# A gated, quantized feed-forward on one core: inner seven-product splits for two of each slot's products in the last batch, with the work around them put anew

## The chip, the cores and the metric

The kernel runs on one core of a Trainium2 chip. Its engines work side by side, each through its own list of instructions in order: TensorE (PE) multiplies 128x128 weights with moving tokens, VectorE (DVE), ScalarE (ACT) and GpSimd (POOL) do the elementwise work, and SyncE (SP) issues the transfers. The metric is the device time of one execution in microseconds; the time before is the median of three runs.

## The reference

For x of 4 batches x 1024 tokens x 512 and a condition vector of 128 per batch, with up weights of 4096x512 and down weights of 512x2048:

```python
scale = cond @ norm_w.T + 1.0
ms = mean(x * x, axis=-1, keepdims=True)
h = x * (scale[:, None, :] * rsqrt(ms + 1e-6))
u = h @ up_w.T
val, gate = split(u, 2, axis=-1)
h = val * gelu(gate, approximate=False)
hq = act_quant(h)        # per token: s = 127/clip(max|h|, 1e-5); clip(round(h*s), -128, 127)/s
wq = weight_quant(down_w)  # ternary, with one scale for the matrix
y = hq @ wq.T
return y + x
```

## The kernel before, in words

The work goes batch by batch (b = 0 to 3), each of 1024 tokens in two halves of 512. A batch has 16 slots, one for every 128 gate columns and the 128 value columns that go with them; slot g is number g mod 16 of batch g // 16. Slots 48 to 63 are the last batch.

In a slot the up-projection of a 2x2 block matrix is done with seven products in place of eight (Strassen's scheme in Winograd's form). Tokens and weights are kept as sums and differences, each as a high and a low fp16 part, so a product c is six matmuls of 512 columns (`product`, L703): two weight parts by two token parts without low by low, times two blocks of the inner dimension. The methods of `Slot` name them: `first` (c = 0) starts bank A; `fourth` (c = 4) starts bank E; `second`, `third`, `fifth`, `gate` and `value` add to A, E and B, a copy of A. A slot has 42 matmuls of 512 columns. `slot` writes them in this order: first, fourth and second of the current slot, third of the one before, fifth, gate of the one before, value. `third_out` (L840) and `value_out` (L860) multiply value by gelu(gate) into the buffer H; `gate_sum` (L848), `value_sum` (L857) and the copies lie between.

The weights of a slot come from a DRAM scratch (s_dram) into one of two buffers, SXY, some of them through a transposing DMA (L489) and some plain (L491), all in SP's queue. The tokens of the next batch, in R, are written by four "turns" per batch (L678), transposing DMAs on the same queue.

While a batch's slots run, DVE and ACT quantize the batch before. `pair_max` takes the maximum over two slots (L906, L911, then L913); `token_max` brings the maximum over the partitions together on POOL (L927); `token_scale` (L932, L938) makes 1/scale on 128x512 numbers; then H is scaled (L993) and rounded, either on DVE (L997) or by two passes of ACT (L1001, L1005). A planner (`Filler`) hands these to the places x, y and z of a slot by their costs, after the due place of each. z is the end of the slot. The quantized batch is multiplied with the ternary weights (also with seven products, `Pair`; L1049 to L1058 make sums, L1070 the matmuls, L1118 the evictions) in slots 10 to 13 of batches 1 and 2, and for batch 2 after slot 63: this last stretch is called the tail. There the last batch's maximum, scale and rounding are done too, with `token_row`, which moves the maxima to 16 partitions by 32 (L949), `token_fold`, which scales them there (L955, L956), and a broadcast over the partitions (L962). The ending matmuls are po_end (L1022).

PSUM has banks by tag: A, E (two each), B (one), and "po" (three), which the down-projection uses.

Of the kernel before, what the change touches and what calls it, by code (L numbers as in the profile page):

```python
# [19 lines left out]
P = 128  # L20
# [7 lines left out]
X_UP = 2.0**8  # L28
# [23 lines left out]
def glu_quant_kernel(  # L52
# [33 lines left out]
    DVE.memset(undo_up, 1.0 / W_UP)  # L86
# [406 lines left out]
    LOADS = ((Y_TO, C_ALL), (0, Y_FROM, True), (Y_FROM + 1, Y_TO), (Y_FROM, Y_FROM + 1, True))  # L493

    def s_load_x(g):
        s_load(g, *LOADS[0])
        s_load(g, *LOADS[1])

# [199 lines left out]
    def product(c, g, ps, start, stop):  # L698
# [3 lines left out]
        for n, (w, l, k) in enumerate(TERMS):  # L702
# [98 lines left out]
    class Slot:  # L801

        def __init__(self, g):
            self.g = g

        def first(self):
            self.A = bank("A", 2, name=f"A_{self.g}")
            product(0, self.g, self.A, True, True)

        def first_copy(self):  # L810
            self.B = bank("B", 1, name=f"B_{self.g}")
            ACT.copy(self.B, self.A)  # L812

        def fourth(self):
            self.E = bank("E", 2, name=f"E_{self.g}")
# [20 lines left out]
        def third(self):  # L836
            product(3, self.g, self.A, False, True)
# [6 lines left out]
        def gate(self):  # L844
            product(2, self.g, self.E, False, True)
# [13 lines left out]
        def value_out(self):  # L859
            DVE.scalar_tensor_tensor(  # L860
                h_half(self.g, 1), self.v, gain(self.g, 0), self.t2, ALU.mult, ALU.mult
            )

# [88 lines left out]
    def token_fold(h, few):  # L952

        row = wpool.tile([P, TOK], F32, name=f"row_{h}", tag="gm", bufs=1)[0:1]
# [35 lines left out]
    def quant_scale(b, i, h, s):  # L990
        v, _ = grid_of(b, i, h)
        r = s[:, h * TOK : (h + 1) * TOK].rearrange("p (o t) -> p o t", o=1)
        DVE.tensor_tensor(v, v, r.to_broadcast([P, 2, TOK]), ALU.mult)  # L993
# [551 lines left out]

    state = {}
    for b in range(1, B):
# [8 lines left out]
        last_pair = NJ // 2 - 1  # L1556
        for h in range(2):
            add_pair(
                dve, act, b - 1, last_pair, h, (0, "xz"[h]),
                lambda now, h=h: token_max(b - 1, h, am),  # L1560
            )
        for h in range(2):
            for cost, f in token_scale(h, am):
# [3 lines left out]
        add_pieces(dve, act, b - 1, am, PIECES, (2, "x"))  # L1567
        for i in range(NJ // 2 - 1):
            for h in range(2):
                add_pair(dve, act, b, i, h, (2 * i + 3, "x"))  # L1570
        steps = {}
        pairs = {}
        if b == 1:
            steps[1, "z"] = [(d_total, (0.1, 0))]
        if b + 1 < B:
# [25 lines left out]
        for j in range(NJ):  # L1601
            g = b * NJ + j
            down = b + 1 < B and j in DOWN
# [12 lines left out]

            def run(p):
                nonlocal left
                for f, _ in steps.get((j, p), ()):
# [4 lines left out]
                elif p == "z":  # L1624
                    left = dve.run((j, p), left)
                if p != "z":
# [18 lines left out]
            if j + 1 == min(DOWN):  # L1645
                mid[0] = more_sums
            if down:
# [201 lines left out]
```

## Time and profile before

| | |
|---|---|
| median of 3 runs | 712.53 us (711.96 to 712.65) |
| span of the profiled execution | 710.3 us |
| outside the span | 2.23 us against the median |
| PE, DVE, ACT, POOL busy | 703.8, 593.1, 421.9, 155.0 us |
| matmuls of 512 columns in a slot of the last batch | 42 |

The page is of one profiled execution. Each row of the groups gives a line, an engine, an operation, what it writes and reads with shapes, how many there are, their busy time with the mean of one in ns, and the idle time before them with what ended it. Rows of a timeline give the start, the length and the same description.

### The profile page before, as it was taken

What the parts mean: (1) busy time and instruction counts of PE and PEld (TensorE: products, weight loads), DVE (VectorE), ACT (ScalarE), POOL (GpSimd) and SP (SyncE); (2) the same over time, 40 slices, a digit from 0 to 9 for tenths busy, and PEclk for the clock granted to TensorE, in tenths of its full rate; (3) what the DMA queues carried; (4) which work ended last, traced back from release to release, by engine and by line L of the source; (5) the groups of instructions that cost most, each with busy time, mean ns of one, the idle gap of its engine ahead of it and who ended that gap; (6) DMA issues with size and microseconds to landing.
All of it is one profiled execution on the core that took longest, in us unless ns stands there. A gap on an engine that the chain in (4) does not pass through costs nothing.

```text
span 710.3 us, 10162 instructions
## 1 busy us (share of the span) xinstructions
PE 703.8 (99%) x3620; PEld 355.3 (50%) x3620; DVE 593.1 (84%) x881; ACT 421.9 (59%) x714; POOL 155.0 (22%) x162
## 2 busy tenths in 40 slices
PE   8999999999999999999999999999999999999998
PEld 4544444444444446664444446665444444445854
DVE  7999878899888799998798868977688888755896
ACT  6987798975777754534336675544334665332473
POOL 1444535551200405430200033440020000000120
PEclk9999999999999999999999999999999999999999
DMA  7989999899776766479344555786744444442253
GB/s 261 324 270 252 254 188 263 217 207 227 264 135 163 179 178 172 136 174 225 118 118 105 133 126 150 191 188 141 207 105 105 104 105 97 99 101 90 105 178 119
DMA packets 223188, 120.26 MB, mean 169 GB/s; under 512 B 185353, under 2 KB 194589, under 8 KB 223138
## 3 DMA queue, kind: packets, MB, share of 16 engines
q1 hardware_dynamic: 222986, 119.49, 65.7%
q8 instruction: 28, 0.46, 0.3%
q14 instruction: 22, 0.18, 0.1%
q10 hardware_dynamic: 152, 0.13, 0.1%
HBM read 52.32 MB, written 23.09 MB: 106 GB/s over the span
## 4 chain that ended last, share of the span: by engine, by line
PE 97%; DVE 1%; ACT 1%; DMA 1%; issue 0%; ACTq 0%; SPq 0%
PE A L703 43%; PE E L703 21%; PE B L703 11%; PE po L1070 9%; PE po_end L1022 4%; PE pg L718 3%; PE pv L718 3%; PE pz L1194 1%; DMA s_dram<-s_rows 1%; PE ptx L1178 1%; PE pv L791 0%; PE po_B L1070 0%; PE pg L791 0%; PE pw L388 0%; PE po_E L1070 0%
## 5 line engine op out<-in xcount | busy, mean ns | idle before, releaser
L703 PEld LDWEIGHTS <-SXY 128*128 128x128 f16 x2268 | 221.9, 98 | 260.3
L703 PE MATMUL A<-R,SXY 128*128 128x512 f16 x1170 | 270.7, 379 | 0.0
L703 PE MATMUL E<-R,SXY 128*128 128x512 f16 x606 | 147.1, 379 | 0.0
L840 DVE SCALAR_TENSOR_TENSOR H<-A,sg,t 128x512 f32<-128x512 f32 x59 | 44.2, 749 | 61.2 <-PE A L703 56.9
L703 PE MATMUL B<-R,SXY 128*128 128x512 f16 x324 | 78.8, 379 | 0.0
L993 DVE TENSOR_TENSOR H<-H,am 128x1024 f32<-128x1024 f32 x64 | 76.5, 1217 | 0.0
L851 ACT ACTIVATE t<-t,sg 128x512 f32<-128x512 f32 x59 | 42.5, 719 | 57.0 <-DVE t L848 56.9
L911 DVE TENSOR_REDUCE gm<-H 128x512 f32<-128x1024 f32 x56 | 69.3, 1237 | 1.0
L927 POOL PARTITION_ALL_REDUCE am<-R x8 | 14.3, 1793 | 228.8 <-DVE R L913 228.8
L834 ACT ACTIVATE t<-B,sg 128x512 f32<-128x512 f32 x59 | 40.5, 686 | 36.9 <-PE B L703 36.9
L827 ACT COPY t<-A 128x512 f32<-128x512 f32 x59 | 34.3, 581 | 43.3 <-PE A L703 42.5
L820 ACT COPY v<-E 128x512 f32<-128x512 f32 x59 | 34.6, 586 | 33.5 <-PE E L703 30.0
L860 DVE SCALAR_TENSOR_TENSOR H<-v,sg,t 128x512 f32<-128x512 f32 x59 | 47.1, 800 | 7.3 <-ACT t L851 6.9
L812 ACT COPY B<-A 128x512 f32<-128x512 f32 x59 | 33.8, 573 | 32.4 <-PE A L703 32.0
L857 DVE TENSOR_TENSOR v<-A,v 128x512 f32<-128x512 f32 x59 | 40.4, 685 | 14.9 <-PE A L703 13.0
L1070 PE MATMUL po<-wd,R 128*128 128x256 fp8e4 x416 | 52.4, 273 | 0.0
L1070 PEld LDWEIGHTS <-R 128*128 128x128 bf16 (+1 forms) x448 | 43.8, 98 | 8.9
L848 DVE TENSOR_TENSOR t<-E,t 128x512 f32<-128x512 f32 x59 | 39.9, 678 | 6.6 <-PE E L703 6.6
L913 DVE TENSOR_TENSOR R<-R,gm 128x512 f32<-128x512 f32 x56 | 41.7, 745 | 1.1
L578 POOL TENSOR_SCALAR ssq<-ssq 128x2 f32<-128x2 f32 x12 | 5.4, 451 | 164.1 <-ACT xt L608 116.1
L1001 ACT ACTIVATE H<-H 128x1024 f32<-128x1024 f32 x33 | 34.7, 1051 | 5.2 <-DVE H L993 5.2
L1005 ACT ACTIVATE R<-H 128x1024 bf16<-128x1024 f32 x33 | 34.8, 1056 | 0.7
(249 smaller groups left out, 928.2 us busy)
## 6 DMA issues: line engine op xcount, KB each, us to landing
SXY<-s_dram SPq DMA_DIRECT2D x45, 256.0 KB, 3.0
SXY<-s_dram SPq DMA_DIRECT2D x51, 128.0 KB, 3.1
xr<-in_x_dram SPq DMA_DIRECT2D x19, 256.0 KB, 3.0
out_dram<-xr SPq DMA_DIRECT2D x19, 256.0 KB, 2.6
H<-in_L_cond_up_w_dram SPq DMA_DIRECT2D x9, 512.0 KB, 4.3
H<-in_x_dram SPq DMA_DIRECT2D x8, 512.0 KB, 6.2
s_dram<-s_rows SPq DMA_DIRECT2D x16, 256.0 KB, 2.7
s_dram<-SXY SPq DMA_DIRECT2D x4, 896.0 KB, 4.5
```

The lines of the kernel that those rows point to most:

```text
L703: PE.matmul(o, s[:, w, k, :], operand(g // NJ, c, l, k), start=start and n == 0, stop=stop and n == len(TERMS) - 1, skip_group_check=True,)
L718: PE.matmul(ps, a[k // 2][:, w, k % 2, :], XP[:, l, k, h * TOK : (h + 1) * TOK], start=n == 0, stop=n == len(terms) - 1,)
L834: ACT.activation(self.t1, self.B, AF.Gelu, scale=gain(self.g, 1))
L840: DVE.scalar_tensor_tensor(h_half(self.g, 0), self.A, gain(self.g, 0), self.t1, ALU.mult, ALU.mult)
L848: DVE.tensor_tensor(self.t2, self.E, self.t2, ALU.add)
L851: ACT.activation(self.t2, self.t2, AF.Gelu, scale=gain(self.g, 1))
L857: DVE.tensor_tensor(self.v, self.A, self.v, ALU.add)
L860: DVE.scalar_tensor_tensor(h_half(self.g, 1), self.v, gain(self.g, 0), self.t2, ALU.mult, ALU.mult)
L911: DVE.tensor_reduce(gm[0], v, AX.X, ALU.max, apply_absolute_value=True)
L913: return [largest, lambda: DVE.tensor_tensor(m, m, gm[0], ALU.max)]
L993: DVE.tensor_tensor(v, v, r.to_broadcast([P, 2, TOK]), ALU.mult)
L1070: PE.matmul(po, w[:, j], m, start=start and j == 0, stop=stop and j == n - 1, skip_group_check=True,)
```

## The change

1. *Slots 4 to 13 of the last batch, in five pairs.* Products 0 and 4 of two neighbouring slots are four blocks with the same tokens. A second seven-product scheme goes over them: two slots by two halves of the inner dimension, two halves of the 512 tokens. A product is then three matmuls of 256 columns, and the two products of two slots, before 24 matmuls of 512 columns, are 42 of 256 (`Inner`, `two_slots`). Sums of tokens are made once for the batch (`two_tokens`); sums of weights for every pair on POOL, with a cast by ACT between (`two_weights`); the raw weights come by transfers of their own (`two_load`). `lower_left` and `lower_right` are additions of 256 columns on DVE. `p0` stands for product 0 of a pair, `p4` for product 4. The steps of both slots' other products are written out by hand in `two_slots`.
2. *A hand-written plan for the last batch.* TWO_PLAN names the slot and place of each piece of quantization in place of the planner. Four scalings go to POOL ("pool scale", L1238), two maxima are taken over four slots at once ("four"), rounds go to ACT ("up", "down"). One maximum (slots 12 and 13, second half) is moved behind slot 63, ahead of `token_fold`.
3. *The third batch's token scales* are made as the tail does it: a row of 16 by 32 numbers, scaled there and broadcast by POOL.
4. *The first weight sums* of the pairs, with their loads and the first token sums, are made at the end of batch 2.
5. Slot 62 takes its banks A and E from the "po" banks; the scale of the tokens X_UP goes from 2^8 to 2^7, and `undo_up` with it.

On SP, at the end of batch 2. Before:

```order
L1113 DMA out_0_dram<-xr_1_1_3_4544 128x512
L678 DMA_TRANSPOSE R_78<-nx_3_2_4602 128x28x128
L678 DMA_TRANSPOSE R_78<-H_79 128x28x128
L491 DMA SXY_81<-s_dram_84 128x1024
L491 DMA SXY_81<-s_dram_84 128x1536
```

Now:

```order
L1358 DMA out_0_dram<-xr_1_1_3_4544 128x512
L687 DMA_TRANSPOSE R_78<-nx_3_2_4602 128x28x128
L912 DMA two_r0_4696<-s_dram_84 128x512 x2
L914 DMA_TRANSPOSE two_r1_4697<-s_dram_84 128x4x128 x2
L687 DMA_TRANSPOSE R_78<-H_79 128x28x128
L491 DMA SXY_81<-s_dram_84 128x1024
L491 DMA SXY_81<-s_dram_84 128x1536
```

Four transfers of raw weights now stand between the last two token turns of the last batch, and the loads of slot 48 behind them.

On DVE, around the end of slot 53 (the next pair is 54 and 55). A_53, E_53, v_53 and t2_53 are slot 53's banks and buffers. Before:

```order
L857 TENSOR_TENSOR v_53_5190<-A_53_5174,v_53_5190 128x512
L860 SCALAR_TENSOR_TENSOR H_79<-v_52_5121,sg_3_4828,t2_52_5149 128x512
L993 TENSOR_TENSOR H_79<-H_79,am_2_4830 128x2x512
L997 TENSOR_SCALAR R_78<-H_79 128x4x256
L977 RECIPROCAL dq_3_4831<-dq_3_4831 128x8
L978 TENSOR_SCALAR dq_3_4831<-dq_3_4831,wmean_105 128x8
L840 SCALAR_TENSOR_TENSOR H_79<-A_53_5174,sg_3_4828,t1_53_5198 128x512
L993 TENSOR_TENSOR H_79<-H_79,am_2_4830 128x2x512 x2
L997 TENSOR_SCALAR R_78<-H_79 128x4x256
L848 TENSOR_TENSOR t2_53_5218<-E_53_5183,t2_53_5218 128x512
```

Now, with `lower_left` (L1017) and `lower_right` (L1020) of the next pair:

```order
L872 TENSOR_TENSOR v_53_5149<-A_53_5148,v_53_5149 128x512
L1238 TENSOR_TENSOR H_79<-H_79,am_2_4852 128x2x512
L1242 TENSOR_SCALAR R_78<-H_79 128x4x256
L863 TENSOR_TENSOR t2_53_5287<-E_53_5289,t2_53_5287 128x512
L1017 TENSOR_TENSOR A_55_5330<-Z0_54_5328,uv_54_5332 128x256
L1020 TENSOR_TENSOR A_55_5330<-A_54_5326,uv_54_5332 128x256
L1017 TENSOR_TENSOR v_55_5331<-Z4_54_5327,two_n_4695 128x256
L1020 TENSOR_TENSOR v_55_5331<-E_54_5329,two_n_4695 128x256
L875 SCALAR_TENSOR_TENSOR H_79<-v_53_5149,sg_3_4850,t2_53_5287 128x512
L855 SCALAR_TENSOR_TENSOR H_79<-A_53_5148,sg_3_4850,t1_53_5301 128x512
```

and on POOL, which had nothing at this place, between the weights of two pairs (two_r1 holds the sums, two_w0 and two_n their two parts):

```order
L960 TENSOR_TENSOR two_n_4695<-two_r1_4697,two_n_4695 128x4x128
L1238 TENSOR_TENSOR H_79<-H_79,am_2_4852 128x2x512
L950 TENSOR_TENSOR two_r1_4697<-two_r0_4696 128x512
L951 TENSOR_TENSOR two_r1_4697<-two_r1_4697 128x128
L952 TENSOR_TENSOR two_r1_4697<-two_r1_4697 128x128
L953 TENSOR_TENSOR two_r1_4697<-two_r1_4697 128x128
L954 TENSOR_TENSOR two_r1_4697<-two_r1_4697 128x128
L960 TENSOR_TENSOR two_w0_4694<-two_r1_4697,two_w0_4694 128x4x128
```

Slot 53's gate sum (before L848, now L863) stands directly behind a scaling and a rounding, and four 256-wide additions follow it; a scaling and the sums of the next weights are on POOL.

On DVE in the tail, around the first `token_fold`. Before:

```order
L1118 SCALAR_TENSOR_TENSOR xr_2_0_0_5921<-po_3_0_0_5928,dq_3_4831,xr_2_0_0_5921 128x512
L1049 TENSOR_TENSOR sr_0_5526<-R_78 128x1024
L955 TENSOR_SCALAR few_0_5959<-few_0_5959 16x32
L956 RECIPROCAL few_0_5959<-few_0_5959 16x32
L1118 SCALAR_TENSOR_TENSOR SXY_81<-po_3_1_E_5982,dq_3_4831,SXY_81 128x256 x2
```

Now:

```order
L1363 SCALAR_TENSOR_TENSOR xr_2_0_0_6165<-po_3_0_0_6172,dq_3_4853,xr_2_0_0_6165 128x512
L1294 TENSOR_TENSOR H_79<-R_78 128x1024
L1155 TENSOR_REDUCE gm_3_6_1_6263<-H_79 128x512
L1157 TENSOR_TENSOR R_78<-R_78,gm_3_6_1_6263 128x512
L1200 TENSOR_SCALAR few_0_6203<-few_0_6203 16x32
L1201 RECIPROCAL few_0_6203<-few_0_6203 16x32
L1363 SCALAR_TENSOR_TENSOR SXY_81<-po_3_1_E_6226,dq_3_4853,SXY_81 128x256 x2
```

A maximum of two slots and its merging stand between the sum and the fold.

The diff, cut to its core:

```diff
-X_UP = 2.0**8
+X_UP = 2.0**7
...
         def first(self):
-            self.A = bank("A", 2, name=f"A_{self.g}")
+            if self.g == LAST * NJ + TWO.stop:
+                self.A, self.E = (po_bank(f"{n}_{self.g}") for n in "AE")
+            else:
+                self.A = bank("A", 2, name=f"A_{self.g}")
             product(0, self.g, self.A, True, True)
...
+    def two_load(c, m):
+        r, n = two_raw(c, m), PLACE[c]
+        for i in range(2):
+            j = block(LAST * NJ + 2 * m + i)
+            d = s_dram[j, :, n * 2 * HALF : (n + 1) * 2 * HALF]
+            if c == 0 or j in TURNED:
+                SP.dma_start(out=r[:, i].rearrange("p w f -> p (w f)"), in_=d)
+            else:
+                SP.dma_start_transpose(r[:, i].rearrange("p w (k f) -> p (w k) f", k=2), d)
...
+        g = two["v"] if m == TWO_1 else two["g"]
+        g = g.rearrange("p (n f) -> p n f", n=4)
+        a11, a12, a21, a22 = (g[:, n] for n in range(4))
+        w = g.rearrange("p (j k) f -> p j (k f)", j=2)
+        def sums():
+            eng.tensor_tensor(w, r[:, :, 0], r[:, :, 1], ALU.add)
+            eng.tensor_tensor(a11, a11, a21, ALU.subtract)
+            eng.tensor_tensor(a21, a21, a22, ALU.add)
+            eng.tensor_tensor(a22, a22, a11, ALU.subtract)
+            eng.tensor_tensor(a12, a12, a22, ALU.subtract)
...
+    class Inner:
+        def __init__(self, c, m, Z, out, uv):
+            self.c, self.m, self.Z, self.out = c, m, Z, out
+            self.u, self.v = uv[:, 0], uv[:, 1]
+        def weight(self, name, w):
+            if name in IN_W:
+                return two["W", self.c][:, IN_W.index(name), w]
+            r = two_raw(self.c, self.m)[:, int(name[1]) - 1, w]
+            return r.rearrange("p (k f) -> p k f", k=2)[:, int(name[2]) - 1]
+        def tokens(self, name, l):
+            if name in IN_T:
+                v = two["T", self.c][:, IN_T.index(name), l]
+                return v.rearrange("p (a t) -> p a t", t=P)
+            h, k = int(name[2]) - 1, int(name[1]) - 1
+            return t_view(LAST)[:, 2 * h : 2 * h + 2, self.c, l, k, :]
+        def product(self, a, b, bank, half, start=False):
+            o = bank[:, half * HALF : (half + 1) * HALF].rearrange("p (a t) -> p a t", t=P)
+            for n, (w, l) in enumerate(((1, 0), (0, 1), (0, 0))):
+                PE.matmul(
+                    o, self.weight(a, w), self.tokens(b, l), start=start and n == 0, stop=n == 2,
+                    skip_group_check=True,
+                )
+        def first(self):
+            self.product("A11", "B11", self.Z, 1, True)
+            self.product("S3", "T3", self.Z, 0, True)
+        def first_copy(self):
+            m1 = self.Z[:, HALF:].rearrange("p (y o) -> p y o", y=1).to_broadcast([P, 2, HALF])
+            ACT.copy(self.out.rearrange("p (y o) -> p y o", y=2), m1)
+            ACT.copy(self.v, self.Z[:, :HALF])
+        def second(self):
+            self.product("A22", "T4", self.Z, 0)
+            self.product("S2", "T2", self.out, 1)
+            self.product("A12", "B21", self.out, 0)
+        def second_copy(self):
+            ACT.copy(self.u, self.out[:, HALF:])
+        def third(self):
+            self.product("S1", "T1", self.out, 1)
+        def lower_left(self, o):
+            DVE.tensor_tensor(o[:, :HALF], self.Z[:, :HALF], self.u, ALU.add)
+        def lower_right(self, o):
+            DVE.tensor_tensor(o[:, HALF:], self.out[:, HALF:], self.v, ALU.add)
+        def fourth(self):
+            self.product("S4", "B22", self.out, 1)
...
+        e.A = po_bank(f"A_{g}")
+        z4 = po_bank(f"Z4_{g}")
+        z0 = po_bank(f"Z0_{g}")
+        e.E = bank("E", 2, name=f"E_{g}")
+        o.A = bank("A", 2, name=f"A_{g + 1}")
...
+        p0.first()
+        p4.first()
+        p0.first_copy()
+        p4.first_copy()
+        prev.gate()
+        prev.gate_sum()
+        run("x")
+        p0.second()
+        p4.second()
+        w0[0]()
+        p0.second_copy()
+        p4.second_copy()
+        if more:
+            two_load(4, m + 1)
+        p0.third()
+        p0.lower_left(o.A)
+        p0.lower_right(o.A)
+        prev.third(0, 3)
+        p4.third()
+        p4.lower_left(o.v)
+        p4.lower_right(o.v)
+        prev.gate_gelu()
+        p0.fourth()
+        prev.third(3, 6)
+        e.first_copy()
+        w0[1]()
+        p4.fourth()
+        w4[0]()
+        prev.value_out()
+        prev.third_out()
+        run("y")
+        e.fifth()
+        e.fifth_copy()
+        e.v = two["v"]
+        ACT.copy(e.v, e.E)
+        e.second()
+        e.second_gelu()
+        run("z")
+        e.value()
+        e.value_sum()
+        o.first_copy()
+        if m + 2 < TWO.stop // 2:
+            two_load(0, m + 2)
+        even("loads")
+        e.gate()
+        e.gate_sum()
+        ran("x")
+        o.fifth()
+        o.fifth_copy()
+        o.E = bank("E", 2, name=f"E_{g + 1}")
+        ACT.copy(o.E, o.v)
+        e.gate_gelu()
+        e.value_out()
+        w4[1]()
+        o.second()
+        o.second_gelu()
+        ran("y")
+        e.third()
+        e.third_out()
+        o.value()
+        o.value_sum()
+        ran("z")
+        odd("loads")
...
+        gm = wpool.tile([P, TOK], F32, name=f"gm_{LAST}_{i}_{h}", tag="gm", bufs=1)
+        DVE.tensor_reduce(gm, v, AX.X, ALU.max, apply_absolute_value=True)
+        m = m_view(LAST, h)
+        DVE.tensor_tensor(m, m, gm, ALU.max)
...
+    TWO_PLAN = [
+        (2, "z", "piece", (0, 0)), (3, "x", "piece", (0, 1)),
+        (3, "z", "piece", (1, 0)), (4, "y", "scale", (1, 1)), (3, "z", "pool scale", (2, 1)),
+        (4, "y", "piece", (2, 0)), (5, "x", "max", (0, 0), (0, 1)), (5, "z", "piece", (3, 0)),
+        (6, "y", "piece", (4, 0)), (7, "x", "four", (1, 0)), (7, "z", "scale", (4, 1)),
+        (8, "y", "piece", (5, 0)), (9, "x", "four", (1, 1)), (9, "z", "scale", (5, 1)),
+        (10, "y", "piece", (6, 0)), (11, "x", "four", (3, 0)), (11, "z", "piece", (7, 0)),
+        (11, "z", "round", (7, 1)),
+        (12, "y", "old", (2, 0)), (13, "x", "four", (3, 1)), (13, "z", "old", (0, 0)),
+        (14, "", "old", (1, 0)), (14, "z", "max", (5, 0), (5, 1)), (15, "x", "max", (6, 0)),
+        (5, "z", "pool scale", (3, 1)), (7, "z", "pool scale", (6, 1)),
+        (9, "z", "pool scale", (7, 1)),
+        (5, "x", "rounds", (1, 1)), (5, "y", "up", (2, 1)),
+        (7, "x", "down", (2, 1)), (7, "x", "up", (3, 1)), (7, "y", "down", (3, 1)),
+        (9, "x", "rounds", (4, 1)), (9, "y", "up", (6, 1)),
+        (11, "x", "down", (6, 1)), (11, "x", "up", (5, 1)), (11, "y", "down", (5, 1)),
+    ]
...
-            for cost, f in token_scale(h, am):
+            for cost, f in token_scale(h, am) if b < LAST else ():
...
+            def fold(h, am=am):
+                row[h] = token_fold(h, few[h], m_view(LAST - 1, h)[0:1])
+                POOL.partition_broadcast(am[:, h * TOK : (h + 1) * TOK], row[h], P)
+            first = two_tokens(0, DVE)
+            steps[0, "x"] = [(first[2], (0, 1.06))]
+            steps[0, "y"] = [(first[3], (1.25, 0))]
+            steps[1, "x"] = [(lambda: row_of(0), (0, 0)), (whole, (1.25, 0)), (sums, (1.9, 0))]
+            steps[1, "y"] = [(high, (0, 1.06))]
+            steps[1, "z"] = [
+                (lambda: row_of(1), (0, 0)), (lambda: fold(0), (0.4, 0)), (lambda: fold(1), (0.4, 0)),
+                (low, (1.25, 0)),
+            ]
+            steps[2, "x"] = [(ws[0], (1.7, 0))]
+            steps[2, "y"] = [(ws[2], (0, 0.6))]
+            steps[2, "z"] = [(ws[3], (0.7, 0))]
...
+            if b + 2 == B and j == NJ - 2:
+                two_places()
+                for c in (0, 4):
+                    two_load(c, TWO_1)
+                fs, ws = two_tokens(0, DVE), two_weights(0, TWO_1)
+                steps.setdefault((14, "y"), []).append((ws[0], (0, 0)))
+                steps[15, "x"] = [(ws[1], (0, 0.6))]
+                steps[15, "y"] = [(get_ready, (0, 0))]
+                steps[15, "z"] = [(fs[0], (1.25, 0)), (fs[1], (1.8, 0))]
...
         old[3].sum1(spare[0])
+        largest(last - 1, 1, am)
         row = token_fold(0, few)
```

190 lines of the change are left out of this document (164 added, 26 removed).

## Prediction

> **What bounds the kernel now.** I read the page first (span, busy shares, the slices, the chain that ended last), then the waits of PE, then the stages one by one.
>
> ```profile
> span 710.3 us, 10162 instructions
> PE 703.8 (99%) x3620; PEld 355.3 (50%) x3620; DVE 593.1 (84%) x881; ACT 421.9 (59%) x714; POOL 155.0 (22%) x162
> PE   8999999999999999999999999999999999999998
> PEclk9999999999999999999999999999999999999999
> PE 97%; DVE 1%; ACT 1%; DMA 1%; issue 0%; ACTq 0%; SPq 0%
> ```
>
> PE is busy in every slice, its clock is full throughout, and 97% of the chain is PE. The median of the runs is 712.53 and the profiled span 710.3, so 2.23 us lie outside the span; I sum against the span and add them back. In the waits of PE from 300 us on the view has its heading and no row, and the stretch of the last batch's slots is full:
>
> ```profile
> engine line waited for: us in total, times, longest us
> 503.00:639.00 136.00, 136.00 (x632) 61.63 (x631) 107.54 (x138) 63.73 (x93) 3.94 (x3) 1.00 0.46 109
> ```
>
> The columns are length, then PE, PEld, DVE, ACT and POOL busy. So a microsecond of matmul taken out of this stretch is a microsecond won, until an engine that PE waits for is late. DVE (107.54 of 136) is the only one near.
>
> **The matmuls.** The chain, and the timeline of the tail, give the pitch for both widths:
>
> ```profile
> 642.07 2.59 PE A L703 x12
> 670.74 7.86 PE po L1070 x72
> L703 PEld LDWEIGHTS <-SXY 128*128 128x128 f16 x2268 | 221.9, 98 | 260.3
> ```
>
> N=512 costs 2.59/12 = 0.216, N=256 costs 7.86/72 = 0.109: half, although each matmul has its own weight load of 98 ns. The second row is of fp8 weights and bf16 tokens; no fp16 matmul of N=256 is in the trace, but 0.216 of the fp16 one is twice 0.109, so the type does not show. In a pair of slots, products 0 and 4 were 24 matmuls: 24 x 0.2158 = 5.18. They become 2 x 7 x 3 = 42 of N=256: 42 x 0.1092 = 4.59. That is 0.59 less a pair, 2.97 in five. The bounds are 2.94 and 3.24 (0.216 halved exactly is 0.108, 42 of them 4.53). I take **-2.97**.
>
> The Trainium skill, "TensorE: Matmul & The Clock Gate", section "Back-to-back issue gap", gives 81 ns for a pair of load and matmul at N=128 and 131 at N=512. A line between them, an estimate, is 98 at N=256, by which the pair would go from 3.14 to 4.12 and the change would lose 4.9 us. The trace differs, with 216 and 109.
>
> **What is added beside it.** ACT gets about ten copies a pair, at most 0.6 each by its rows (573 for 128x512 on the page), 30 us in five pairs on top of 63.73 of 136: hidden. DVE gets four PSUM sums of 256 columns a pair, some 0.4 each (half of 683 and a start), 8 us; it loses two token scalings with their eight reciprocals, and four scalings go to POOL.
>
> ```profile
> L938 DVE RECIPROCAL am<-am 128x128 f32<-128x128 f32 x8 | 7.0, 921 | 0.1
> L932 DVE TENSOR_SCALAR am<-am 128x512 f32<-128x512 f32 x2 | 0.8, 390 | 0.0
> L993 DVE TENSOR_TENSOR H<-H,am 128x1024 f32<-128x1024 f32 x16 | 19.2, 1218 | 0.0
> L997 DVE TENSOR_SCALAR R<-H 128x1024 bf16<-128x1024 f32 x7 | 4.9, 694 | 0.2
> L857 DVE TENSOR_TENSOR v<-A,v 128x512 f32<-128x512 f32 x16 | 10.9, 683 | 3.7 <-PE A L703 3.1 <-issue 0.5
> L913 DVE TENSOR_TENSOR R<-R,gm 128x512 f32<-128x512 f32 x14 | 9.7, 689 | 0.3
> ```
>
> Minus 7.8 and minus 4.9 against plus 8: DVE's total stays. X_UP and undo change constants, no time. The third batch's scales now go through a row, a fold and a broadcast. The tail does that already:
>
> ```profile
> 660.17 0.63 SPq L949 DMA_DIRECT2D few<-am  x1
> 664.36 1.09 POOL L962 PARTITION_BROADCAST am<-row  x1 [4.22 <-DMA row<-few]
> ```
>
> That is 5.3 us from row to end. Here it runs from slot 1 to the last third of slot 2, more than a slot of 9.07 (136/15): hidden; were it late, DVE's scaling at the end of slot 2 would wait, with that slot's rounding behind it. What is left to cost is where DVE, SP and POOL are late at one place.
>
> **The seam from batch 2 to batch 3.** SP now issues, one after the other:
>
> ```profile
> 493.21 5.53 SPq L678 DMA_TRANSPOSE R<-nx  x1
> 498.83 3.58 SPq L678 DMA_TRANSPOSE R<-H  x1
> 502.51 1.48 SPq L491 DMA_DIRECT2D SXY<-s_dram  x3
> 504.04 1.20 SPq L489 DMA_TRANSPOSE SXY<-s_dram  x1
> SXY<-s_dram SPq DMA_DIRECT2D x45, 256.0 KB, 3.0
> 505.93 2.75 PE L703 MATMUL A<-R,SXY 128*128 128x512 f16 x12
> ```
>
> The twelve matmuls from 505.93 hold six of slot 47 and then slot 48's first product, at 505.93 + 6 x 0.216 = 507.23. Its weights are in the load issued at 502.51, landing 3.0 later, at 505.5: 1.7 to spare. The change puts four DMAs (two plain, two transposed, 128 KB each) between the last two token turns, so the last turn and everything behind it on this queue move. Single issues of these two kinds:
>
> ```profile
> 581.40 0.57 SPq L491 DMA_DIRECT2D SXY<-s_dram  x1
> 582.02 1.19 SPq L489 DMA_TRANSPOSE SXY<-s_dram  x1
> ```
>
> Two plain at 0.49 to 0.57 and two transposed at 1.19 are 3.36 to 3.52. The load is then issued at 505.87 and lands at 508.9, 1.65 after slot 48 wants it; the last token turn, which it needs too, ends its issue at 505.8. Nothing else is between PE and this wait, so it is a stall: **+1.65**. Lower bound 0.6: two such turns held SP for 5.53 and 3.58, so part of a turn's issue is waiting for transfers, and half of that difference may come back once others stand ahead of it. Upper bound 2.3: the engines share the added 512 KB, and the load takes a fifth longer to land. On ACT the cast of the first weights waits for POOL's sums and can hold slot 47's copy behind it by one copy (573 ns); that lies inside the same stall, and costs 0.6 without it.
>
> **The seams between pairs.** POOL now makes weight sums and one 128x1024 scaling a pair. What POOL does to DVE shows early in the trace:
>
> ```profile
> 127.47 1.15 POOL L463 TENSOR_TENSOR s_rows<-H,s_rows 128x512 f16<-128x512 f32 x1
> 127.74 1.44 DVE L913 TENSOR_TENSOR R<-R,gm 128x512 f32<-128x512 f32 x1
> L727 POOL TENSOR_TENSOR H<-R 128x1024 f32<-128x1024 f16 x2 | 4.4, 2214 | 0.0
> L848 DVE TENSOR_TENSOR t<-E,t 128x512 f32<-128x512 f32 x16 | 10.9, 679 | 3.6 <-PE E L703 3.6
> ```
>
> The DVE maximum that takes 0.689 alone took 1.44 and ended 0.56 after POOL's instruction: it stood still beside it. So a POOL scaling can cost DVE up to 2.21, a first weight sum up to 1.15. The Trainium skill, "SBUF — State Buffer", section "Who interferes with whom", says the same of two-input DVE work on SBUF and spares DVE work with one such input; the first half agrees with 1.44 against 0.689, the second no row here settles.
>
> How late may DVE be? From a pair's start PE has p0.first and p4.first (12 x 0.109 = 1.31), the old slot's gate (1.30), two seconds (18 x 0.109 = 1.96), p0.third (0.33), half of the old third (0.65) and p4.third (0.33): p0.fourth may start at 5.88. Before it DVE does the gate sum (0.68, from 2.61 + 0.2), and two 256-wide sums, the second after p0.third: 4.90 + 0.2 + 0.4 = 5.50. Slack is 0.38, and the gate sum itself can start 1.5 late before that counts. Behind DVE's value sum in slot 53 stand a scaling and a rounding (1.22 + 0.69), done at about 0.2 + 0.68 + 1.91 = 2.8 after the pair's start: just in time without POOL. POOL's scaling there stands behind its own weight low, which comes in the middle of the odd slot, so most of its 2.21 falls before the seam. I charge one seam (slot 54, the only one with scaling and rounding on DVE and a scaling on POOL) with half of 2.21 + 0.38 - 1.9 = 0.7: **+0.3**. Bounds 0 and 3.9, the upper at three seams of 1.3 (2.21 less 1.5, and 2.21 + 1.15 less 1.5, in the mean).
>
> Slot 62's first product now takes banks that the down-projection's use left free and waits for slot 60's output (0.75): **+0.1** (0 to 0.3).
>
> **The tail.** The second half's maximum of slots 60 and 61 moves ahead of the token fold, 1.24 + 0.69 = 1.93 on DVE:
>
> ```profile
> 660.60 0.68 DVE L1049 TENSOR_TENSOR sr<-R 128x1024 bf16<-128x1024 bf16 x1
> 661.96 0.17 DVE L955 TENSOR_SCALAR few<-few 16x32 f32<-16x32 f32 x1 [0.68 <-DMA few<-am]
> 663.44 0.75 DVE L1118 SCALAR_TENSOR_TENSOR xr<-po,dq,xr 128x512 f32<-128x512 f32 x1 [0.24 <-PE po L1070]
> 677.58 0.73 DVE L1118 SCALAR_TENSOR_TENSOR SXY<-po,dq,SXY 128x512 f32<-128x512 f32 x1
> 678.43 1.89 PE L1022 MATMUL po_end<-wd,R 128*128 128x512 fp8e4 x8
> ```
>
> Two idle stretches take up 0.68 + 0.24; the rest, 1.01, stays with DVE, which is back to back to 677.58. The eviction there frees a bank at 678.31 that PE wants with the third matmul of po_end, at 678.86: slack 0.55. **+0.45**, bounds 0 and 1.0.
>
> **Sum:** -2.97 + 1.65 + 0.3 + 0.1 + 0.45 = -0.47. Span 709.8, time 712.53 - 0.47 = **712.1**, taken as 712.0.
>
> **The rivals.** *Covered.* The transfers land early enough and the tail absorbs its second: the losses shrink to 0.6 + 0.1 + 0 = 0.7, or to nothing, and the time is 709.6 to 710.9, about 710.3. For it speaks that single loads in the quieter stretch are short and that PE had no wait at all; against it, that the 3.4 us on SP exceed the 1.7 that are spare. *POOL against DVE.* Scaling and first weight sum meet DVE's chain ahead of p0.fourth at three seams: 3 x 1.3 in place of 0.3, +3.6, so 715.7. It decides from 1.5 us of DVE lateness at the gate sum. For it speaks the 1.44 row, and DVE at 107.54 of 136 with little room; against it POOL's place in the order. *Weight loads pace the short matmuls.* If half a load (49 ns) came out into the open, a pair's 42 would cost 42 x 0.158 = 6.64, 1.46 more than before: +7.3 in place of -2.97, 722.3. The 72 matmuls of 7.86 us speak against it. It breaks even at 5.18/42 = 0.123.
>
> **How the numbers follow.** Forecast 0.42, covered 0.34, POOL against DVE 0.20, weight loads 0.02, something else slower 0.02. What a measurement of this kernel can tell from no change is about 0.2%, 1.43 us. The forecast's own range is 711.0 to 714.1 (the seam's 0.6 to 2.3, the tail's 0 to 1, a second seam), of which 0.02 falls on each side of 1.43. So faster 0.34 + 0.02 = 0.36, same 0.38, slower 0.26. The range 709.8 to 715.1 holds the forecast, most of the covered case and the lower part of the POOL case.
>
> **What would show it.** PE's waits, empty before, get a row of about 1.6 us at slot 48's first product, released by a DMA; if not, that term falls. At the pairs, waits of p0.fourth on DVE's 256-wide sum: at slot 54 alone by the forecast, at 52, 54, 56, 58 by the POOL case, with DVE scalings and value outs of 1.3 us and more beside POOL's rows. The 42 short matmuls of a pair should take 4.59. In the tail, a wait of about 0.45 on a DVE eviction at po_end. The forecast is wrong if batch 3's slots 48 to 61 are not some 3 us shorter without stalls, or if PE waits by more than 3.5 us in all.

## The result and the profile after

The changed kernel took 719.85 us (median of 4 runs, 719.11 to 720.20), against 712.25 for the kernel before beside it (711.94 to 712.65): a ratio of 1.011, 95% interval 1.0095 to 1.0124. That is 7.6 us slower, outside the predicted range of 709.8 to 715.1. The profiled execution has a span of 717.8 us (710.3 before).

The page of the changed kernel, the rows that answer to those shown of before:

```profile
span 717.8 us, 10531 instructions
PE 703.3 (98%) x3710; PEld 364.5 (51%) x3710; DVE 617.7 (86%) x904; ACT 434.0 (60%) x750; POOL 215.3 (30%) x222
PE   8999999999999999999999999999899988999998
PEclk9999999999999999999999999999999999999999
PE 88%; DVE 7%; DMA 2%; ACT 1%; POOL 1%; issue 0%; SPq 0%; ACTq 0%; DVEq 0%; POOLq 0%
```

DVE now has 7% of the chain that ended last, about 50 us, in a kernel where it had 1%; that is how long the chain runs along DVE, not what DVE costs. The waits of PE from 480 us on, where there had been none (in total, times, longest):

```profile
PE Z L991 <- ACT uv L1003: 4.0, 2, 2.0
PE A L712 <- ACT t L842: 1.5, 2, 0.8
PE A L712 <- DMA SXY<-s_dram: 1.3, 1, 1.3
PE A L991 <- DVE A L1020: 0.5, 2, 0.3
```

In the timeline these are seven waits: 0.83 at slot 47's value and 1.33 at slot 48's first product (the seam between the batches), 0.66 in pair 52, 0.30 in pair 54, 1.99 in pair 56, 1.99 in pair 58, 0.16 in pair 60. By the starts of PE's rows, each costs about 0.16 more than the wait shows: the rows of pair 56 run to 583.33 + 0.33 + 6 x 0.216 = 584.95, and the next starts at 587.11, a gap of 2.16 for a wait of 1.99. (The profile counts a wait from the end of the last row, and the row of one 512-wide matmul, 0.379 on the page, ends 0.16 behind the pitch of 0.216.) So the waits cost 7.26 + 7 x 0.16 = 8.38.

The short matmuls kept their pitch, the time from one start to the next (the chain at the start of pair 52):

```profile
546.16 1.31 PE Z L991 x12
```

1.31 / 12 = 0.109, so the gain of 2.97 is there. What the waits don't explain is the clock. Windows of 1 us around the second long wait (after the length come PE, PEld, DVE, ACT and POOL busy; then the granted clock):

```profile
606.00:607.00 1.00, 0.21 (x2) 0.19 (x2) 1.00 (x2) 1.00 (x3) 0.84 (x3) 1.00 0.42 90
607.00:608.00 1.00, 1.00 (x8) 0.71 (x6) 1.00 (x2) 0.53 (x2) 1.00 (x1) 0.56 0.00 0
608.00:609.00 1.00, 1.00 (x6) 0.68 (x5) 0.36 (x1) 0.34 (x1) 0.84 (x3) 0.50 0.00 0
609.00:610.00 1.00, 1.00 (x7) 0.72 (x5) 0.43 (x1) 0.04 (x1) 0.14 (x1) 0.50 0.00 0
610.00:611.00 1.00, 1.00 (x8) 0.66 (x7) 0.06 (x1) 0.41 (x2) 0.00 (x0) 0.73 0.00 0
611.00:612.00 1.00, 1.00 (x9) 0.70 (x8) 0.78 (x3) 0.58 (x1) 0.00 (x0) 1.00 0.03 8
```

PE was granted half its clock directly behind the wait: by the means of 0.56, 0.50, 0.50 and 0.73 for 0.88, 1, 1 and 0.54 us, about 3.4 in all. By the starts of its rows that cost 1.66 (4.57 us of work from the end of the wait took 6.23). The account closes to 0.1: -2.97 + 8.38 + 1.66 = +7.07, and the last matmul ends at 714.29 instead of 707.14, 7.15 later.

Where the two long waits come from is read in the chain of waits at pair 56:

```profile
577.37 0.69 DVE t L863
578.06 3.65 DVE gm L1804
581.74 0.95 DVE R L1806
582.68 2.76 DVE H L875
585.45 0.67 DVE H L855
586.20 0.57 ACT A L1002
586.77 0.30 ACT uv L1003
587.11 0.49 PE Z L991 x3
```

L863 is slot 54's gate sum, L1804 and L1806 the maximum over four slots and its merge, L875 slot 54's value output, L855 its third output. The third output is the last reader of a "po" bank, and the pair's first copy (L1002) writes the same bank: three banks go round, and each pair takes three. PE waits for the copy right behind it (L1003). Two pieces are long: 3.73 for the four-slot maximum, which before does not have, and 2.84 for a value output that takes 0.75 alone. The second has its reason on POOL. The low part of the next weights (L960) lies beside the merge, and the scaling, next in POOL's list, began while the merge still ran, so it was ahead of the value output, which ended 0.56 after it:

```profile
580.98 1.16 POOL L960 TENSOR_TENSOR two_n<-two_r,two_n 128x512 f16<-128x512 f32 x1 [2.84 <-ACT two_n L957]
582.61 2.84 DVE L875 SCALAR_TENSOR_TENSOR H<-two_n,sg,t 128x512 f32<-128x512 f32 x1
582.09 2.80 POOL L1238 TENSOR_TENSOR H<-H,am 128x1024 f32<-128x1024 f32 x1
```

At the seam, SP's queue and PE's two waits:

```profile
498.80 1.00 SPq L912 DMA_DIRECT2D two_r<-s_dram  x2
499.90 2.51 SPq L914 DMA_TRANSPOSE two_r<-s_dram  x2
502.50 3.54 SPq L687 DMA_TRANSPOSE R<-H  x1
506.09 1.52 SPq L491 DMA_DIRECT2D SXY<-s_dram  x3
506.95 1.45 PE L712 MATMUL A<-R,SXY 128*128 128x512 f16 x6 [0.83 <-ACT t L842]
509.73 1.47 PE L712 MATMUL A<-R,SXY 128*128 128x512 f16 x6 [1.33 <-DMA SXY<-s_dram]
```

### The profile page after: what moved, and what is told of

It is laid out like the page before. It is cut to its first block, busy times and chain, and to the rows that moved or that the text cites. A ratio compares the mean times of both kernels' runs of the same rounds, so it can differ in the third digit from the quotient of the medians.

```text
span 717.8 us, 10531 instructions
## 1 busy us (share of the span) xinstructions
PE 703.3 (98%) x3710; PEld 364.5 (51%) x3710; DVE 617.7 (86%) x904; ACT 434.0 (60%) x750; POOL 215.3 (30%) x222
## 4 chain that ended last, share of the span: by engine, by line
PE 88%; DVE 7%; DMA 2%; ACT 1%; POOL 1%; issue 0%; SPq 0%; ACTq 0%; DVEq 0%; POOLq 0%
PE A L712 37%; PE E L712 18%; PE B L712 10%; PE po L1315 9%; PE po_end L1267 4%; PE pg L727 3%; PE pv L727 3%; DVE gm L1804 2%; DVE H L875 1%; DMA SXY<-s_rows 1%; PE A L991 1%; PE pz L1439 1%; PE E L991 1%; DMA s_dram<-s_rows 1%; PE Z L991 1%; PE ptx L1423 1%
## 5 line engine op out<-in xcount | busy, mean ns | idle before, releaser
L712 PEld LDWEIGHTS <-SXY 128*128 128x128 f16 x2148 | 210.1, 98 | 245.3 <-issue 2.1
L712 PE MATMUL A<-R,SXY 128*128 128x512 f16 x1110 | 259.5, 379 | 2.8 <-ACT t L842 1.5
L712 PE MATMUL E<-R,SXY 128*128 128x512 f16 x546 | 132.5, 379 | 0.0
L855 DVE SCALAR_TENSOR_TENSOR H<-A,sg,t 128x512 f32<-128x512 f32 x59 | 44.1, 748 | 43.3 <-PE A L712 40.7
L1238 DVE TENSOR_TENSOR H<-H,am 128x1024 f32<-128x1024 f32 x60 | 78.1, 1320 | 0.0
L1155 DVE TENSOR_REDUCE gm<-H 128x512 f32<-128x1024 f32 x48 | 59.4, 1237 | 0.8
L872 DVE TENSOR_TENSOR v<-A,v 128x512 f32<-128x512 f32 x54 | 37.0, 685 | 15.4 <-PE A L712 13.5
L875 DVE SCALAR_TENSOR_TENSOR H<-v,sg,t 128x512 f32<-128x512 f32 x54 | 42.2, 782 | 5.7 <-ACT t L866 5.3
L835 ACT COPY v<-E 128x512 f32<-128x512 f32 x49 | 28.7, 586 | 26.1 <-PE E L712 24.7
L863 DVE TENSOR_TENSOR t<-E,t 128x512 f32<-128x512 f32 x59 | 40.1, 681 | 5.2 <-PE E L712 5.0
L1157 DVE TENSOR_TENSOR R<-R,gm 128x512 f32<-128x512 f32 x48 | 36.3, 757 | 1.1
L1246 ACT ACTIVATE H<-H 128x1024 f32<-128x1024 f32 x30 | 31.6, 1052 | 4.2 <-DVE H L1238 3.9
L712 PEld LDWEIGHTS <-R 128*128 128x128 f16 x210 | 20.5, 98 | 26.1 <-issue 1.6
```

Of the source, the lines that this page charges most:

```text
L712: PE.matmul(o, s[:, w, k, :], operand(g // NJ, c, l, k), start=start and n == 0, stop=stop and n == len(TERMS) - 1, skip_group_check=True,)
L855: DVE.scalar_tensor_tensor(h_half(self.g, 0), self.A, gain(self.g, 0), self.t1, ALU.mult, ALU.mult)
L863: DVE.tensor_tensor(self.t2, self.E, self.t2, ALU.add)
L872: DVE.tensor_tensor(self.v, self.A, self.v, ALU.add)
L875: DVE.scalar_tensor_tensor(h_half(self.g, 1), self.v, gain(self.g, 0), self.t2, ALU.mult, ALU.mult)
L1155: DVE.tensor_reduce(gm[0], v, AX.X, ALU.max, apply_absolute_value=True)
```

## The experiments

Two theories on the long waits were set against each other: *lock*, by which DVE's work with two inputs in SBUF stands still beside POOL's, so that the third output comes late; and *maximum*, by which DVE's list with the 3.73 us of the four-slot maximum is too long whatever POOL does. A third question was the seam, a fourth the clock.

One execution differs from another in its first 170 us, by up to 1.7 us (POOL's first reduction over the partitions starts between 166.2 and 167.9). Single profiles are therefore compared by the stretch from POOL's second reduction of the batch before last, near 350 us, to the end: 359.8 before (710.3 - 350.5), 367.3 with the change (717.8 - 350.5). Versions below for which no ratio is given were executed once.

**The loads moved.**

```diff
-                for c in (0, 4):
-                    two_load(c, TWO_1)
+                two_load(0, TWO_1)
...
+            if b == LAST and j == 0:
+                two_load(4, TWO_1)
```

> Edit: the two transposed loads of product 4's raw weights are moved from between the last two token turns to the start of slot 48. Theory SP (the four extra loads delay slot 48's own load): SP's queue gets back about 2.5 us, the wait of slot 48's first product on the DMA (1.33 us in the changed kernel) goes to 0; the other wait of this seam, 0.83 us of slot 47's value product on the ACT copy, stays. Span 717.8 - 1.5 = 716.3. Rival (the seam waits for ACT and POOL, and the DMA would be late anyway): span unchanged, the DMA wait stays above 1.

The wait on the DMA was gone. The other was 1.36, where 0.83 was expected to stay: on ACT slot 47's copy stands behind the cast, and the cast waits for the last of POOL's sums.

```profile
504.99 0.45 POOL L954 TENSOR_TENSOR two_n<-two_n 128x128 f32<-128x128 f32 x1
505.47 0.62 ACT L957 CAST two_w<-two_n 128x512 f16<-128x512 f32 x1 [3.31 <-POOL two_n L954]
```

That this edit made it longer is not shown: in the five other versions that keep the change's seam it was 0.93 to 1.90, and the wait behind it 0.20 to 0.83, in one of them put down to DVE; together they were 1.35 to 2.39, against 2.16 in the changed kernel. Span 714.0, stretch 364.3. The two long waits were there, 1.99 each, and the clock stayed full behind them; that is 1.66 of the 3.0 by which the stretch is shorter.

**The loads moved and the cast behind the copy.**

```diff
-                steps[15, "x"] = [(ws[1], (0, 0.6))]
-                steps[15, "y"] = [(get_ready, (0, 0))]
+                steps[15, "y"] = [(ws[1], (0, 0.6)), (get_ready, (0, 0))]
```

> Edit: the two loads moved as in the run before, and the cast of the first weights on ACT put behind slot 47's copy instead of ahead of it. Theory SP plus ACT order: no wait of PE at slots 47 and 48 (0.83 + 1.33 in the changed kernel, 1.36 with the loads alone moved); pairs as in the changed kernel. Span 714.0 - 1.5 = 712.5. Rival (the seam waits for the token turn, not for loads and casts): one wait of about a microsecond stays.

No wait at slots 47 and 48, neither here nor in the four versions below that keep both edits; stretch 362.7, 1.6 less than with the loads alone. The seam's cost is shown to be these two together: the queue of SP and the order on ACT. The cast was not moved without the loads, so how the cost is shared between them is open.

**POOL's scalings ahead**, in three slots, then in one alone and in the other alone.

```diff
-        (5, "z", "pool scale", (3, 1)), (7, "z", "pool scale", (6, 1)),
-        (9, "z", "pool scale", (7, 1)),
+        (5, "x", "pool scale", (3, 1)), (7, "x", "pool scale", (6, 1)),
+        (9, "x", "pool scale", (7, 1)),
```

> Edit: in slots 53, 55 and 57 POOL does its 128x1024 scaling ahead of the second weights' low part, so that it falls beside DVE's long maximum over four slots and not beside the value output behind it. Theory lock (DVE's value output stands still while POOL scales, and the third output behind it holds the bank that the next pair's first copy wants): both stalls of 2.0 us, at the pairs 56 and 58, go, and the dip of the clock after the second with them: span 717.8 - 4.3 - 1.7 = 711.8. Rival maximum (the four-slot maximum of 3.73 us alone makes the third output late): the stalls stay above 1.3 us each, span above 715.

714.19 us, ratio 1.0034 (1.0021 to 1.0046); the clock stayed full. The long waits fell from 1.99 to 0.80 and 0.79: neither to nothing, as *lock* had it, nor above 1.3, as *maximum* had it. That the span, 712.1, is near the 711.8 of *lock* is chance: 0.9 of it is the shorter start of this execution. DVE and POOL in pair 56:

```profile
576.40 3.78 DVE L1804 TENSOR_REDUCE gm<-H 128x512 f32<-128x2048 f32 x1
581.05 1.64 DVE L875 SCALAR_TENSOR_TENSOR H<-two_n,sg,t 128x512 f32<-128x512 f32 x1
577.08 2.37 POOL L1238 TENSOR_TENSOR H<-H,am 128x1024 f32<-128x1024 f32 x1
579.41 1.17 POOL L960 TENSOR_TENSOR two_n<-two_r,two_n 128x512 f16<-128x512 f32 x1
580.65 1.48 POOL L950 TENSOR_TENSOR two_r<-SXY 128x512 f32<-128x512 f16 x1
```

POOL's scaling now lies beside the maximum, which takes 3.78 beside it against 3.73. But POOL's list moves up: the first of the next weight sums (L950) is now beside the value output.

> Edit: only slot 55's POOL scaling is put ahead. Theory lock: the stall at pair 56 goes, the one at 58 stays at 2.0. For the clock: if a dip needs two stalls within some 20 us, there is none here and the span is about 713.9; if one stall of 2 us is enough, the clock dips behind pair 58 and the span is about 715.6.

> Edit: only slot 57's POOL scaling is put ahead. Theory lock: the stall at pair 58 goes, the one at 56 stays at 2.0. For the clock: no dip if it needs two stalls (span about 713.9), a dip behind pair 56 if one is enough and its phase decides (715.6).

With slot 55's alone the waits were 0.79 and 1.98, with slot 57's alone 1.99 and 0.80 (stretches 364.1 and 363.6). Of each long wait 1.2 us belong to the scaling of its own pair. No dip of the clock in either; but two such waits had no dip behind them in the two runs on the seam above, so neither of the two rules for the clock is shown.

**Four-slot maxima as pairs.**

```diff
-(7, "x", "four", (1, 0))
+(7, "x", "max", (1, 0), (2, 0))
...
-(9, "x", "four", (1, 1))
+(9, "x", "max", (1, 1), (2, 1))
...
-(11, "x", "four", (3, 0))
+(11, "x", "max", (3, 0), (4, 0))
...
-(13, "x", "four", (3, 1))
+(13, "x", "max", (3, 1), (4, 1))
```

> Edit: the four maxima over four slots are each made as two over two slots with a merge each, in the same places; POOL's scalings stay where the change has them. Measured so far: the four-slot maximum takes 3.73 us, with POOL beside it or not, a two-slot one 1.24. Theory lock with a race for the port: DVE's chain ahead of the value output is 0.6 shorter (3.86 for 4.42), it reaches the value output about when POOL comes to its scaling, and the stalls at pairs 56 and 58 are either gone or still near 2, as the one or the other comes first. Rival maximum: each stall is shorter by 0.6, to 1.4, whatever POOL does.

Both waits 1.98, and the clock full behind them; span 717.1, stretch 366.3.

```profile
581.89 1.42 DVE L1157 TENSOR_TENSOR R<-R,gm 128x512 f32<-128x512 f32 x1
583.24 2.83 DVE L875 SCALAR_TENSOR_TENSOR H<-two_n,sg,t 128x512 f32<-128x512 f32 x1
581.61 1.16 POOL L960 TENSOR_TENSOR two_n<-two_r,two_n 128x512 f16<-128x512 f32 x1 [2.17 <-ACT two_n L957]
582.73 2.80 POOL L1238 TENSOR_TENSOR H<-H,am 128x1024 f32<-128x1024 f32 x1
```

The 0.6 saved in DVE's list came back as standing beside POOL: the second merge came 0.28 behind the start of POOL's low part and took 1.42, and the scaling began before the merge had ended and was ahead of the value output again. *Maximum* alone, with its 1.4, falls; *lock* had allowed for this outcome and for the opposite one.

**POOL's low part ahead, too**: the second weights' cast before the gate's gelu on ACT, with the scalings ahead.

```diff
+        w4[1]()
         e.gate_gelu()
         e.value_out()
-        w4[1]()
```

> Edit: POOL's scalings ahead as before, and the cast of the second weights ahead of the gate's gelu on ACT, so that POOL's low part, too, falls beside DVE's long maximum. Theory lock: what was left of the two stalls (0.8 each) was the value output waiting for that low part (1.56 us for 0.75); now it takes 0.75 and the waits at pairs 56 and 58 are under 0.1: span 712.1 - 1.9 = 710.2. Rival maximum: 0.8 each stays, since DVE's own list is as long as before.

A miss: waits of 1.27 and 0.74 at pairs 56 and 58, and a new one of 0.37 at pair 52; stretch 363.4, 0.9 longer than without the move. The move could not bring the low part forward. In both versions it follows POOL's scaling without a gap, so the cast was not what it waited for, and what lay beside the value output was the next weight sum (L950), as the rows above show. At pair 56 POOL's list even ran some 0.5 later against DVE's, as its first sum waited for a load.

```profile
579.12 2.37 POOL L1238 TENSOR_TENSOR H<-H,am 128x1024 f32<-128x1024 f32 x1
581.45 1.16 POOL L960 TENSOR_TENSOR two_n<-two_r,two_n 128x512 f16<-128x512 f32 x1
```

**All repairs.** The edits above at the seam, the scalings and the cast, and in pair 52 the first weights' cast and the second weights' sums behind the fifth copy.

```diff
         e.first_copy()
-        w0[1]()
+        if m > TWO_1:
+            w0[1]()
         p4.fourth()
-        w4[0]()
+        if m > TWO_1:
+            w4[0]()
...
         e.fifth_copy()
+        if m == TWO_1:
+            w0[1]()
+            w4[0]()
```

> Edit: loads and cast at the seam as in the seam run, POOL's scalings and the second weights' casts as in the run beside it, and in the pair 52 the first cast behind the fifth copy. If the gain of the short matmuls is the 2.97 us that the pitch gives and all the rest were the stalls named, PE waits below 0.5 us behind slot 47 and the span is 710.3 - 2.97 + 0.4 = 707.7, the time 710.0, ratio 0.9965. If a further cost hides behind the stalls, the time stays above 711.5.

712.09 us, ratio 0.9999 (0.9990 to 1.0008): no difference from before, and not the 710.0 expected. PE still waited 0.83 and 0.75 at pairs 56 and 58, and 0.44 at pair 54 for a POOL low part. With 0.16 each that is 2.5 of the 2.97.

**The scalings left out, or on DVE**, in slots 55 and 57, on top of all repairs. In the first only the lines that go are edited, and two pieces of the third batch's quantization are not scaled.

```diff
-        (7, "x", "pool scale", (6, 1)),
-        (9, "x", "pool scale", (7, 1)),
+        (7, "z", "scale", (6, 1)),
+        (9, "z", "scale", (7, 1)),
```

> Edit: the version with all repairs, without POOL's scalings of slots 55 and 57 (two pieces of the third batch's quantization are left out, so these are rounded unscaled). Theory lock: POOL's low part and next sums come 2.4 us sooner, fall wholly beside the maximum, the waits at pairs 56 and 58 (0.83 and 0.75) go: span 709.2 - 1.9 = 707.3. Rival (DVE's own list is too long there): both waits stay at 0.7.

> Edit: the version with all repairs, but slots 55 and 57's scalings are done by DVE at the same place of the plan, behind the value sum, beside the one that is there. Theory lock: the waits of the first copies at 56 and 58 go as without scalings; DVE has 1.22 more ahead of the gate sum, 1.5 of lateness is free there: waits of p0.fourth of 0 to 0.8 each, span 707.5 to 709. Rival (DVE is the bound and POOL's help is needed): both pairs wait over 1.2 us, span above 710.

*Lock* missed in both. Without the scalings the waits were 0.72 and 0.72 (stretch 359.8), the 0.7 of the rival. But DVE's own list was not all of it, as POOL's weight sums had moved up beside the merge and the value output:

```profile
579.41 1.55 DVE L1811 TENSOR_TENSOR R<-R,gm 128x512 f32<-128x512 f32 x1
580.89 0.94 DVE L875 SCALAR_TENSOR_TENSOR H<-two_n,sg,t 128x512 f32<-128x512 f32 x1
579.26 1.16 POOL L950 TENSOR_TENSOR two_r<-SXY 128x512 f32<-128x512 f16 x1
```

With DVE doing them they were 0.71 and 0.72, and 0.41 came at p0.fourth of pair 56: 713.07 us, ratio 1.0012 (1.0003 to 1.0021). Both versions also kept a wait of 0.46 at pair 54, on POOL's low part. So the scaling accounts for 1.2 of each long wait and not for the 0.8 that is left. By the rows that rest needs both DVE's long list before the third output and POOL work beside its two-input steps: merge and value output take 0.86 and 0.19 longer than alone (0.69 and 0.75), more than the 0.72. No version took POOL's work away from there altogether, so this is worked out and not tested.

**The merge out of the chain.** All repairs, slot 53's scaling back at its place, and the merges at the end of their slots (the plan's line for one of the four is shown).

```diff
-        m = m_view(LAST, h)
-        DVE.tensor_tensor(m, m, gm, ALU.max)
+        gms[i, h] = gm
...
+    def merge(i, h):
+        m = m_view(LAST, h)
+        DVE.tensor_tensor(m, m, gms[i, h], ALU.max)
...
-(7, "x", "four", (1, 0)), (7, "z", "scale", (4, 1)),
+(7, "x", "four", (1, 0)), (7, "z", "merge", (1, 0)), (7, "z", "scale", (4, 1)),
```

> Edit: the version with all repairs, with two moves more: the merge behind each four-slot maximum goes to the end of its slot, behind the value sum, and slot 53's POOL scaling is back at its place. Measured before: with all repairs PE still waits 0.83 and 0.75 at the pairs 56 and 58, since POOL's next weight sums stand beside the merge and the value output (1.64 for 0.75). Theory lock: with the merge's 0.9 out of the chain to the third output both waits are under 0.15, the wait of 0.44 on POOL at pair 54 goes and one of 0.3 at its fourth product comes; span 709.2 - 1.7 = 707.5, ratio 0.997. Rival (what is taken out here is given back at the gate sum, behind the merge): waits of p0.fourth on DVE of 0.5 and more at 56 and 58, span 709.

710.23 us, ratio 0.9973 (0.9963 to 0.9984), 8 runs: faster than both kernels. One wait is left from 480 us on, at pair 54:

```profile
PE A L991 <- DVE A L1020: 0.5, 1, 0.5
```

Stretch 357.9: 1.9 less than before, of the 2.36 that -2.97 + 0.45 + 0.16 gives; the rest of 0.5 is not accounted for. In pair 56 the value output still stood beside POOL (1.69 for 0.75), but had room for it. The rival, that the merge is given back at the gate sum, falls: there is no wait at p0.fourth of 56 or 58. Two things were moved at once; the waits at 56 and 58 are laid to the merge, as slot 53's scaling comes ahead of pair 54.

## Why the prediction was wrong

**The matmuls, -2.97:** right. The pitch is 0.109 with fp16 weights as with fp8, and the rival of weight loads as the pace has no row for it.

**The seam, +1.65:** right in mechanism and place, under-sized. Slot 48's load was issued at 506.09 (505.87 was said) and landed 3.6 later (3.0 was said), so 0.8 over the term; the real cost is 2.48 (2.16 of waits and 2 x 0.16), beyond its upper bound of 2.3. That the late copy of slot 47 costs nothing beside it was right. What it costs by itself once the DMA is out of the way was larger than said, 1.36 + 0.16 for 0.6: the term counted the cast's own length and not its wait for POOL's five sums, which began at 501.83, when their loads had landed, and ended at 505.44. The one sum that stood beside DVE (0.78 for 0.45) is 0.3 of it.

**The seams between pairs, +0.3 with an upper bound of 3.9:** this step failed. The waits of pairs 52 to 60 cost 5.10 + 5 x 0.16 = 5.9, and all seven waits are 7.26, twice the 3.5 that was named as the sign of being wrong. The step followed one wait, p0.fourth behind DVE's 256-wide sums; that one was real and small (0.30 at pair 54, 0.16 at 60). The wait that decided was the first copy of a pair on the bank that the third output of the slot two before still reads. It was not on the list because the step asked when DVE's sums are late, not which bank each product of the new pair reuses and who reads it last. The pair's second products had been counted as free to start behind the old gate.

**"DVE's total stays":** it didn't. DVE was busy for 107.54 us from 503 to 639 before; the same work takes 143 us now and keeps it busy for 123.88:

```profile
503.00:646.00 143.00, 135.74 (x721) 71.02 (x720) 123.88 (x151) 75.54 (x130) 62.84 (x64) 0.99 0.46 107
```

By its groups of rows there, some 15 us of this are rows that are longer than alone: 12 scalings of 1.72 in the mean for 1.22, 10 rounds of 1.11 for 0.69, five value outputs of 1.58 for 0.75, four merges of 0.88 for 0.69. Sums of tokens and of the first weights that DVE makes, 10.8 us, were not counted either. Nor was the four-slot maximum priced: it is there four times, takes 3.73, and with its merge it stands between the gate sum and the third output.

**POOL against DVE:** the rival with the right cause, at the wrong place: 715.7 was worked out for p0.fourth. It was given 0.20, on the ground that most of POOL's scaling falls before the seam. It didn't: the low part ahead of it had to wait for ACT's cast (2.84 us idle before it), and the scaling ran from 582.09 to 584.89 where pair 56 begins at 582.35, beside DVE's longest list before a bank that PE wants.

**Slot 62, +0.1 and the tail, +0.45:** no wait at either. In the tail, DVE's eviction ended 0.6 later against po_end than before, not 1.0, about the 0.55 of slack that there was.

**Not in the sum at all:** 1.66 for the clock.

The runs show that the waits are removed by the named edits. That the seam (2.48), the pairs (5.9) and the clock (1.66) less the gain of 2.97 add up to the loss is worked out from the rows of one profile, and closes to 0.1. What set off the dip of the clock stays open.

## What to carry to other kernels

Where products are regrouped, list for each new accumulation the bank it takes, the last reader of that bank, and that reader's place in its engine's queue; the slack that counts is the smallest over all of them. Offloading elementwise work to POOL is not a subtraction from DVE's list: its price is set by which two-input steps of DVE it falls beside, and clearing one place lets POOL's next piece move up to it. Taking a short step out of the chain to the bank's last reader (0.7 us of merge) ended waits of 0.83 and 0.75 that leaving out 2.2 us of POOL work had only brought to 0.72.

## What the hardware showed

**A maximum over four slots is dearer than two over two.** The same 2048 numbers a partition, in groups of four with a stride between them, took 3.73 us against 2 x 1.24, or 3.17 with the second merge of 0.69 that two of them need. Over all runs its executions in the last batch took 3.71 to 3.79, the longest with POOL's scaling beside them. Why is open; no run varied the stride alone.

**POOL slows some one-input work, too.** A rounding from fp32 to bf16 takes 0.69 alone. Beside a sum on POOL it took 1.53:

```profile
567.64 1.53 DVE L1242 TENSOR_SCALAR R<-H 128x1024 bf16<-128x1024 f32 x1
566.48 2.13 POOL L950 TENSOR_TENSOR two_r<-two_r 128x512 f32<-128x512 f16 x1
```

POOL's sum, 1.16 alone, took 2.13; its first half lies beside DVE's scaling, which ended at 567.61, its second beside the rounding. The Trainium skill, "SBUF — State Buffer", section "Who interferes with whom", says that tensor_scalar can use a mode with two ports, which contends, and that a reduction on trn2 never does. The traces agree with both: 1.53 against 0.69, and 3.71 to 3.79 with or without POOL.

**The clock can halve after a wait of 2 us.** In the changed kernel the second of two waits of 1.99 was followed by half the clock for 3.4 us; all four of its runs show a mean clock of 0.997 or 0.998, where every run of the other versions has 0.999 or 1.000. With the loads moved, with the cast moved too, and with pairs of maxima, the same two waits, 20 us apart, were followed by no dip. The Trainium skill, "TensorE: Matmul & The Clock Gate", section "What's actually happening", has a free-running window of 3413 ns in which PE's activity is watched. The length agrees with 3.4 us. That the phase of that window decides which wait is punished would fit. The half clock begins at 607.13 in the trace; counted back from there in steps of 3.41, the second wait (no matmul from 604.64 to 606.79, 2.15 us) lies whole in one step, and the first (584.95 to 587.11) is parted into 1.70 and 0.46. Counted the same way from the clock's last change, no other trace has more than 2.0 us without a matmul in one step from 20 us on, and none has a dip before its end. But no run here moved a wait against the window with all else the same, so it stays open.
